# Scores of the experts as eight more columns of the value and output projections, in an attention and mixture-of-experts layer on one core

## The chip, the cores and the metric

The kernel runs on one core of a Trainium2 chip. The metric is device time in microseconds of one execution, lower is better. The engines that the profile names are TensorE (PE, with its weight loads as PEld), VectorE (DVE), ScalarE (ACT), GpSimd (POOL) and SyncE (SP), which issues most of the DMAs.

## The reference

Two sublayers, each fed with a normalised input, and each with its output normalised before it is added to the residual stream. `x` is 2 x 2048 x 256 in float32, with 4 heads of 64 and 8 experts of 256 x 256.

```python
x = L0_attn_x
x = x + _layernorm(_L0_attn_ref(_layernorm(x, axis=-1), ln_gamma, ..., w_o, b_o), axis=-1)
x = x + _layernorm(_L0_ffn_ref(_layernorm(x, axis=-1), gate_w, expert_w), axis=-1)

# _L0_attn_ref
xn = _layernorm(x, ln_gamma, ln_beta)
q, k, v = proj(w_q), proj(w_k), proj(w_v)          # each xn @ w.T
qn = _rmsnorm(q, q_gamma) * dh ** (-0.5); kn = _rmsnorm(k, k_gamma)
attn = softmax(einsum('bhid,bhjd->bhij', qn, kn))
return merge(einsum('bhij,bhjd->bhid', attn, v)) @ w_o.T + b_o

# _L0_ffn_ref
scores = einsum('bsh,eh->bse', x, gate_w)
onehot = one_hot(argmax(scores, axis=-1), E)
return x + einsum('bsef,bse->bsf', einsum('bsh,efh->bsef', x, expert_w), onehot)
```

Each token goes to the one expert with the highest score. Only the order of a token's eight scores matters, not their size.

## The kernel before

The 4096 tokens are 32 tiles of 128, 16 a batch. Two paths stand behind a branch on the size of the gammas of q and k (`bounded`, computed from `gq_all` and `gk_all`); the inputs take `bounded_path`, and the other path is not run.

Ahead of the branch the weights of q and k are loaded and turned on PE (`turn_weight`, line 148, copied by ACT at line 151), and the constants are made on POOL. `load_x` (line 70) loads four token tiles at a time on SP's queue; the first two of these loads are ahead of the branch.

`bounded_path` records its instructions in an order written out by hand. A generator stands for each job (`project` for a token tile, `tokens` for a tile behind the attention, `expert_weights`, `order`, `places`, `collect`, `block_sums`), and a `yield` ends the piece of work that it puts into one slot. `queue` holds each job with the slot in which it begins; `between(now)` moves every running job by one piece. A slot of the attention is two of the 256 steps: eight score matmul records `s` (line 953), their exponentials `p` on ACT (line 961), DVE's running sum `acc` of the exponentials (lines 996 and 998), and eight records `po` that weigh the values (line 1007). What `between` adds stands between a slot's `s` and its `po` on PE. The engines run their instructions strictly in the order in which they are recorded.

`project` normalises a tile of x, turns it on PE (`pt_x`, line 349), brings it back with ln_gamma and ln_beta as scale and bias on ACT (`xnT`, line 354, one instruction for each half), multiplies it by the weights of q and k (`pqk`, line 364) and of v (`pv`, line 373), and normalises and turns q and k. Tiles of the first batch fill the stretch before the first scores and the first slots; those of the second batch are spread over later slots. `turn_values` and `turn_rest` turn w_v, w_o and gate_w in the first slots (lines 148 and 167).

`tokens` takes a tile when its 512 rows have been attended: output projection `py` (line 700), bias (line 715), layer norm, residual sum `x2`, second layer norm `x2n` (line 731). Then it turns `x2n` (`pt_f`, line 739), copies it back (`xT`, line 747), multiplies it by the gate (`pg`, line 751), and `choose` (lines 176 to 183) makes the one-hot `pick` of the first best score.

Tiles 0 to 15 are group A and 16 to 27 group B. When the last tile of a group has its pick, `order` sorts the group's tokens by expert (`rank`, `src`, some 30 DVE instructions between them), and each `places` job then gathers 128 tokens of one expert (line 605), loads that expert's matrix (line 619), multiplies (`pt_g`, `pe`, lines 627 and 637), normalises and stores them; each `collect` job gathers a tile's results back (line 675) and adds the residual (line 687). The last four tiles, 28 to 31, have no group: they are multiplied by all eight experts (`pe`, line 776) and the picks select (lines 791 and 793).

When the attention is over, `finish` orders what is left by a list schedule with written-out costs: each job gives the engine and an estimate of its next piece in `Next(engine, cost, ...)`, and the piece that can begin first goes next.

Of the kernel before, what the change touches and what calls it, by code (L numbers as in the profile page):

```python
# [9 lines left out]
F32 = mybir.dt.float32  # L10
# [10 lines left out]
GAMMA_MAX = 5.0  # L21


@with_exitstack
def kernel(
# [39 lines left out]
    def load_x(g, pool, tag="xg", bufs=2):  # L65
        if pool:
            xs[g] = pool.tile([P, XG, D], F32, tag=tag, name=f"x{g}", bufs=bufs)
        else:
            xs[g] = xs[g - 2]
        nc.sync.dma_start(  # L70
            out=xs[g],
            in_=x_f[g * XG * P : (g + 1) * XG * P, :].rearrange("(c p) d -> p c d", p=P),
        )
# [5 lines left out]
    gk_all = const.tile([P, DH], F32, tag="gk_all", name="gk_all")  # L79
    nc.sync.dma_start(out=gq_all, in_=q_gamma.partition_broadcast(P))  # L80
# [8 lines left out]
    g_ln = const.tile([P, NCH], F32, tag="g_ln", name="g_ln")  # L89
    b_ln = const.tile([P, NCH], F32, tag="b_ln", name="b_ln")  # L90
    nc.sync.dma_start(out=g_ln, in_=ln_gamma.rearrange("(c p) -> p c", p=P))
    nc.sync.dma_start(out=b_ln, in_=ln_beta.rearrange("(c p) -> p c", p=P))
    load_x(1, store, "xg1", 1)
    early = ctx.enter_context(ExitStack())
    raw = early.enter_context(tc.tile_pool(name="raw_w", bufs=2))
    wq_raw = load_raw(raw, w_q, "wq_raw")
    wk_raw = load_raw(raw, w_k, "wk_raw")

# [7 lines left out]
    nc.gpsimd.memset(half, 0.5)  # L106
    ones = const.tile([P, DH], F32, tag="ones", name="ones")
# [30 lines left out]

    wqkT = const.tile([P, NCH, 2, D], F32, tag="wqkT", name="wqkT")
    wvT = const.tile([P, NCH, D], F32, tag="wvT", name="wvT")  # L140
    woT = const.tile([P, NCH, D], F32, tag="woT", name="woT")
    gateT = const.tile([P, NCH, E], F32, tag="gateT", name="gateT")

# [11 lines left out]
    )  # L155

    idle = psum_w.tile([P, P], F32, tag="idle", name="idle", bufs=1)
    for _ in range(18):
        nc.tensor.transpose(idle, ident, ident)
    for i, (w, name) in enumerate(((wq_raw, "pt_wq"), (wk_raw, "pt_wk"))):  # L160
        pt = psum_w.tile([P, KB // P, P], F32, tag="ps_w", name=name)
        turn_weight(w, pt, wqkT[:, :, i, :], nc.scalar.copy)
    early.close()

    def turn_gate(pt):
        for ic in range(NCH):
            nc.tensor.transpose(
                pt[:, ic, :E], gate_raw[:, ic * P : (ic + 1) * P], ident[:E, :E]
            )
        nc.vector.tensor_copy(gateT, pt[:, :NCH, :E])  # L170
# [15 lines left out]
    def bounded_path():  # L186
# [9 lines left out]
        wv_raw = load_raw(raw, w_v, "wv_raw", nc.sync)  # L196
# [25 lines left out]
        token = route.tile([P, NT], F32, tag="token", name="token")  # L222

        def four(ps):
            return ps.rearrange("p (a c) -> p a c", c=P)

        def turn_values():
            turn_weight(wv_raw, four(ps_m("pt_wv")), wvT)
            yield

        def turn_rest():
            nc.gpsimd.tensor_scalar(g_q8, g_q, DH**-0.5, None, ALU.mult)
            yield
            turn_weight(wo_raw, four(ps_m("pt_wo")), woT)
            turn_gate(four(ps_m("pt_gate")))
# [91 lines left out]
        class Batch:  # L327
            def __init__(self, b):
# [4 lines left out]
                self.V = kv.tile([P, NT, D], F32, tag="V", name=f"V{b}")  # L333

        def project(bt, t):
# [5 lines left out]
            mv, rs = moments(src, f"a{n}")  # L341
# [11 lines left out]
            for c in range(NCH):  # L353
                nc.scalar.activation(  # L354
                    xnT[:, c, :],
                    pt[:, c * P : (c + 1) * P],
                    AF.Identity,
                    bias=b_ln[:, c : c + 1],
                    scale=g_ln[:, c : c + 1],
                )  # L360
# [11 lines left out]
            for c in range(NCH):  # L372
                nc.tensor.matmul(  # L373
                    pv[:, :D],
# [7 lines left out]
            nc.scalar.copy(bt.V[:, t, :], pv[:, :D])  # L382
# [70 lines left out]
        def load_experts():  # L453
            nonlocal weD
            v = kv.tile([P, NT, D], F32, tag="V", name="ring")
            ring.extend(v[:, i : i + NCH, :] for i in range(0, NT, NCH))
# [237 lines left out]
        def tokens(bt, qb, j, oTs, gr):  # L694
# [3 lines left out]
            py = ps_m(f"py{tt}")[:, :D]  # L698
# [9 lines left out]
            if gr:  # L708
                y = wk.tile([P, D], F32, tag="y", name=f"y{tt}", bufs=3)
                xr = wk.tile([P, D], F32, tag="xr", name=f"xr{tt}")  # L710
            else:
                kept = wk.tile([P, HP, KB], F32, tag="p", name=f"kept{tt}", bufs=5)
                x2n, last = kept[:, 0, :D], kept[:, 0, D:]
                y, xr = kept[:, 1, D:], last
            nc.vector.tensor_tensor(y, py, bo, ALU.add)
# [6 lines left out]
            scale, _ = yield from norm(y, f"z{tt}", away, give="m")  # L722
            yield later("DVE", 1.2, give="m" if slot else "")

            x2 = wk.tile([P, D], F32, tag="x2", name=f"x2_{tt}", bufs=4)
            nc.vector.scalar_tensor_tensor(x2, y, scale, xr, ALU.mult, ALU.add)
# [5 lines left out]
            if gr:  # L732
                rows = slice((tt - gr.first) * P, (tt - gr.first + 1) * P)
                nc.sync.dma_start(out=gr.x2[rows, :], in_=x2)
                nc.sync.dma_start(out=gr.x2n[rows, :], in_=x2n)
            yield later("PE", 0.3, take="m")
# [6 lines left out]
            if gr:  # L743
                xT = wk.tile([P, NCH, P], F32, tag="xT", name=f"xT{tt}", bufs=4)
            else:
                xT = kept[:, 1, :D].rearrange("p (c n) -> p c n", n=P)
            nc.scalar.copy(xT, pt[:, :D].rearrange("p (c n) -> p c n", n=P))
            yield later("PE", 0.4, take="m", give="m")
            pg = ps_m(f"pg{tt}")
            for c in range(NCH):  # L750
                nc.tensor.matmul(  # L751
                    pg[:, :E],
                    xT[:, c, :],
                    gateT[:, c, :],
                    start=(c == 0),
                    stop=(c == NCH - 1),
                )
            yield then("DVE", 0.8)
# [679 lines left out]
```

## Time and profile before

| | |
|---|---|
| median of 3 runs | 821.41 us (819.0 to 821.75) |
| the profiled execution | 817.68 us, of which the span of instructions is 815.9 |
| granted TensorE clock, mean over the span | 0.982 |
| first scores `s` | 39.3 us |
| last `po` ends | 732.3 us |
| PE's last matmul ends | 799.5 us |
| `acc` on DVE, one 128x1024 addition | 1.222 us, 224 of them |
| `p` on ACT, one 128x1024 exponential | 1.110 us, 256 of them |

The profile's group lines give, for one line, engine, operation and shape, the count, the busy time and the mean of one instruction, then the engine's idle time before them and what ended it. A float32 matmul shows two records. PE's records overlap, so the distance from one start to the next is the better price of a job in a full slot. In the timeline, a start is followed by the time to the end of that run of equal instructions; brackets hold an idle time before it and its releaser.

### The profile page before, as it was taken

Reading aid. Unit: us, or ns where it says so; the run is one execution under the profiler, and the core shown is the slowest. Engines: PE = TensorE matmul, PEld = TensorE weight load, DVE = VectorE, ACT = ScalarE, POOL = GpSimd, SP = SyncE. Lnnn points to the kernel's source line nnn. Section 1 sums busy time; section 2 is a strip of 40 time slices with the busy share of each in tenths; the row PEclk is TensorE's granted clock in tenths of the full one; section 3 lists DMA queues with packets and bytes.
Section 4 is the critical chain, followed back from the end, with each engine's and each line's share of the span. In section 5 each row is a group of like instructions: output and inputs, shape, how many; then the busy total and the mean of one; then the engine's idle time right before and its main releaser. Section 6 shows DMA issues by size and latency. Waiting matters only on the chain.

```text
span 815.9 us, 10616 instructions
## 1 busy us (share of the span) xinstructions
PE 773.4 (95%) x3328; PEld 336.2 (41%) x3328; DVE 631.3 (77%) x1310; ACT 467.4 (57%) x759; POOL 321.9 (39%) x325
## 2 busy tenths in 40 slices
PE   6999999999999999999999999999999998987991
PEld 4544434433434443433333344444443333334650
DVE  3767788697869778787798978687787988977765
ACT  2776556666665665656645445656656555526750
POOL 3544412153443334242233026667563555236004
PEclk8999999999999999999999999999999999989996
DMA  4001111200100000010311033434221323267136
GB/s 151 27 27 39 52 53 52 65 27 20 46 20 19 20 14 20 7 33 20 103 59 46 18 106 97 125 101 115 72 59 53 98 91 116 78 192 224 50 112 195
DMA packets 48687, 57.60 MB, mean 71 GB/s; under 512 B 6408, under 2 KB 39952, under 8 KB 48624
## 3 DMA queue, kind: packets, MB, share of 16 engines
q1 hardware_dynamic: 42336, 44.91, 17.3%
q0 software_dynamic: 3568, 9.32, 4.6%
q10 hardware_dynamic: 2720, 2.62, 1.1%
q8 instruction: 28, 0.46, 0.2%
q14 instruction: 35, 0.29, 0.1%
HBM read 37.69 MB, written 19.14 MB: 70 GB/s over the span
## 4 chain that ended last, share of the span: by engine, by line
PE 75%; DVE 15%; ACT 3%; DMA 3%; issue 2%; POOL 1%; POOLq 0%; SPq 0%; DVEq 0%; ACTq 0%
PE po L1007 23%; PE s L953 23%; PE pqk L364 6%; DVE acc L998 5%; PE pv L373 3%; PE pe L776 3%; PE py L700 3%; PE peA L637 3%; PE sm L969 2%; DVE acc L977 2%; PE pt_qk L401 2%; PE peB L637 2%; PE pg L751 2%; PE pt_x L349 1%; PE pt_f L739 1%
## 5 line engine op out<-in xcount | busy, mean ns | idle before, releaser
L961 ACT ACTIVATE p<-s,nbound 128x1024 f32<-128x1024 f32 x256 | 271.3, 1110 | 214.6 <-PE s L953 205.1
L998 DVE TENSOR_TENSOR acc<-acc,p 128x1024 f32<-128x1024 f32 x224 | 273.7, 1222 | 12.1 <-ACT p L961 1.2
L953 PE MATMUL s<-QT,KT 64*128 64x512 f32 x1024 | 255.6, 618 | 0.6 <-ACT p L961 0.6
L1007 PE MATMUL po<-p,V 128*64 128x512 f32 x1024 | 250.2, 610 | 0.0
L953 PEld LDWEIGHTS s<-QT,KT 64*128 64x128 f32 x1024 | 88.6, 187 | 163.1 <-issue 96.7
L1007 PEld LDWEIGHTS po<-p,V 128*64 128x64 f32 x1024 | 64.1, 137 | 123.4 <-issue 122.5
L283 POOL TENSOR_TENSOR rn<-rs_t,mhalf 128x8 f32<-128x8 f32 x32 | 58.6, 1832 | 74.3 <-DVE rs_t L282 65.2
L283 POOL TENSOR_TENSOR rs_z<-rs_t,mhalf 128x1 f32<-128x1 f32 x28 | 35.9, 1283 | 86.6 <-DVE rs_t L282 86.6
L283 POOL TENSOR_TENSOR rs_a<-rs_t,mhalf 128x1 f32<-128x1 f32 x32 | 22.9, 715 | 105.6 <-DVE rs_t L282 105.6
L364 PE MATMUL pqk<-wqkT,xnT 128*128 128x512 f32 x128 | 62.6, 612 | 0.6 <-DVE woT L151 0.6
L605 POOL DMA_INDIRECT rows<-x2nA,srcA x23 | 30.7, 1334 | 41.1 <-DMA ring<-weTd 35.9
L283 POOL TENSOR_TENSOR rs_y<-rs_t,mhalf 128x1 f32<-128x1 f32 x28 | 32.7, 1167 | 33.0 <-DVE rs_t L282 32.8
L977 DVE RECIPROCAL acc<-acc 128x128 f32<-128x128 f32 x45 | 42.5, 945 | 0.0
L977 DVE RECIPROCAL acc<-sm 128x128 f32<-128x128 f32 x19 | 18.1, 954 | 26.0 <-PE sm L969 25.9
L675 POOL DMA_INDIRECT fgA<-fnA,posA x16 | 22.4, 1403 | 35.5 <-DVE rs_t L282 11.6
L700 PE MATMUL py<-woT,oT 128*128 128x256 f32 x128 | 34.7, 393 | 0.5 <-ACT xTB L632 0.5
L373 PE MATMUL pv<-wvT,xnT 128*128 128x256 f32 x128 | 32.9, 380 | 0.0
L373 PEld LDWEIGHTS pv<-wvT,xnT 128*128 128x128 f32 x128 | 24.6, 192 | 17.5 <-issue 12.0
L354 ACT ACTIVATE xnT<-pt_x,b_ln,g_ln 128x128 f32<-128x128 f32 x64 | 25.8, 459 | 8.4 <-PE pt_x L349 8.4
L605 POOL DMA_INDIRECT rows<-x2nB,srcB x19 | 19.8, 1044 | 26.9 <-DVE srcB L586 19.3
L283 POOL TENSOR_TENSOR rs_fA<-rs_t,mhalf 128x1 f32<-128x1 f32 x23 | 18.4, 800 | 28.5 <-DVE rs_t L282 28.0
L364 PEld LDWEIGHTS pqk<-wqkT,xnT 128*128 128x128 f32 x128 | 22.4, 195 | 17.4 <-issue 16.4
(234 smaller groups left out, 954.7 us busy)
## 6 DMA issues: line engine op xcount, KB each, us to landing
ring<-weTd SPq DMA_DIRECT2D x34, 256.0 KB, 3.0
x<-in_L_attn_x_dram SPq DMA_DIRECT2D x8, 512.0 KB, 4.2
xr<-in_L_attn_x_dram SPq DMA_DIRECT2D x28, 128.0 KB, 2.2
fnA<-fA SPq DMA_DIRECT2D x23, 128.0 KB, 2.4
fnB<-spare SPq DMA_DIRECT2D x18, 128.0 KB, 1.7
we_raw<-in_L_ffn_expert_w_dram ACTq DMA_DIRECT2D x8, 256.0 KB, 2.6
weTd<-weT SPq DMA_DIRECT2D x8, 256.0 KB, 2.1
x2A<-x SPq DMA_DIRECT2D x16, 128.0 KB, 1.7
```

Of the source, the lines that this page charges most:

```text
L283: nc.gpsimd.tensor_tensor(dst, t[:, :n], mhalf[:, :n], ALU.pow)
L354: nc.scalar.activation(xnT[:, c, :], pt[:, c * P : (c + 1) * P], AF.Identity, bias=b_ln[:, c : c + 1], scale=g_ln[:, c : c + 1],)
L364: nc.tensor.matmul(pqk, xnT[:, c, :], wqkT[:, c, :, :].rearrange("p a d -> p (a d)"), start=(c == 0), stop=(c == NCH - 1),)
L373: nc.tensor.matmul(pv[:, :D], xnT[:, c, :], wvT[:, c, :], start=(c == 0), stop=(c == NCH - 1),)
L605: nc.gpsimd.indirect_dma_start(out=xg, out_offset=None, in_=gr.x2n[:, :], in_offset=bass.IndirectOffsetOnAxis(ap=gr.src[:, j : j + 1], axi ...
L637: nc.tensor.matmul(pe, xT[:, c, :], w[:, c, :], start=(c == 0), stop=(c == NCH - 1))
L700: nc.tensor.matmul(py, oT[:, bass.ts(j, P)], woT[:, c, :], start=(c == 0), stop=(c == NCH - 1),)
L953: nc.tensor.matmul(s[:, r, :], bt.KT[rows, c, bass.ts(kc, P)], bt.QT[qb][rows, c, :], start=True, stop=True,)
L961: nc.scalar.activation(p, s, AF.Exp, bias=nbound)
L977: nc.vector.reciprocal(acc[:, 0, cols], share[:, cols])
L998: nc.vector.tensor_tensor(acc, acc, p, ALU.add)
L1007: nc.tensor.matmul(po[r * DH : (r + 1) * DH, :], batches[b].V[:, kc, h * DH : (h + 1) * DH], p[:, r, :], start=(kc == 0), stop=(kc == NT - 1),
```

## The change

The score of expert e for a token is the product of row e of gate_w with `x2n`. As `x2n` is `x2` less its mean, times a positive factor that all eight scores share, the order of the scores is that of the products of `x2` with the rows of gate_w from which their mean is taken (`gate_c`). `x2` is a sum of the attention's normalised output and of the normalised input, both linear in tensors that the kernel has before: so the changed kernel adds eight columns to the transposed weights of the output projection (`woT`, the product of w_o with the gate) and eight to those of the values (`wvT`, the gate itself), carries them along, and joins them at the end: score = y[256:264] x weight + V[256:264], with weight the ratio of the two scales (`roots` keeps the scale of each token's first norm).

For V's eight columns to be those of the bare normalised input, ln_gamma and ln_beta are no longer applied to it; they go into the weights. `xnT` is `xn` plus a constant 1/16, one ACT instruction for both halves, and `add_shares` rewrites the weights of q, k and v with `share` (128x128 tiles of (16 beta - gamma)/256), one PE product and one DVE instruction for each half. The product of the constant with the rewritten weights gives beta's part.

Of group tiles, `pt_f`, `xT` and `pg` go; the last four tiles keep `pt_f` and `xT`, and lose `pg`. The pick stands right behind `x2`, so a group is complete some slots earlier. `turn_outputs` takes the place of `turn_rest`'s weights and runs in slot 1; w_v is loaded and turned ahead of the branch; g_ln and b_ln are loaded first, and the second load of x behind the branch. The condition for the slots that sort their jobs by age changes.

```diff
+RAISE = 1 / 16
...
+    nc.sync.dma_start(out=g_ln, in_=ln_gamma.rearrange("(c p) -> p c", p=P))
+    nc.sync.dma_start(out=b_ln, in_=ln_beta.rearrange("(c p) -> p c", p=P))
     nc.sync.dma_start(out=gq_all, in_=q_gamma.partition_broadcast(P))
     nc.sync.dma_start(out=gk_all, in_=k_gamma.partition_broadcast(P))
     load_x(0, store, "xg0", 1)
...
-    load_x(1, store, "xg1", 1)
+    xs[1] = store.tile([P, XG, D], F32, tag="xg1", name="x1")
...
-    raw = early.enter_context(tc.tile_pool(name="raw_w", bufs=2))
+    raw = early.enter_context(tc.tile_pool(name="raw_w", bufs=3))
     wq_raw = load_raw(raw, w_q, "wq_raw")
     wk_raw = load_raw(raw, w_k, "wk_raw")
+    wv_raw = load_raw(raw, w_v, "wv_raw")
...
+    dif = const.tile([P, NCH], F32, tag="dif", name="dif")
+    nc.gpsimd.tensor_scalar(dif, b_ln, 1.0 / RAISE, None, ALU.mult)
+    nc.gpsimd.tensor_tensor(dif, dif, g_ln, ALU.subtract)
+    nc.gpsimd.tensor_scalar(dif, dif, 1.0 / D, None, ALU.mult)
+    share = const.tile([P, NCH, P], F32, tag="share", name="share")
+    for c in range(NCH):
+        nc.gpsimd.tensor_scalar(
+            share[:, c, :], ident, 0.0, dif[:, c : c + 1], ALU.mult, ALU.add
+        )
+    nc.scalar.activation(gate_c, gate_raw, AF.Copy, scale=-1.0 / D, accum_out=off)
+    nc.scalar.activation(gate_c, gate_raw, AF.Identity, bias=off)
+    DG = D + E
...
+    for w, name, dst in (
+        (wq_raw, "pt_wq", wqkT[:, :, 0, :]),
+        (wk_raw, "pt_wk", wqkT[:, :, 1, :]),
+        (wv_raw, "pt_wv", wvT[:, :, :D]),
+    ):
         pt = psum_w.tile([P, KB // P, P], F32, tag="ps_w", name=name)
-        turn_weight(w, pt, wqkT[:, :, i, :], nc.scalar.copy)
+        turn_weight(w, pt, dst, nc.scalar.copy)
+    pt = psum_w.tile([P, KB // P, P], F32, tag="ps_w", name="pt_gate")
+    for ic in range(NCH):
+        nc.tensor.transpose(
+            pt[:, ic, :E], gate_c[:, ic * P : (ic + 1) * P], ident[:E, :E]
+        )
+    nc.scalar.copy(gateT, pt[:, :NCH, :E])
+    nc.scalar.copy(wvT[:, :, D:], pt[:, :NCH, :E])
...
+    def add_shares(w, ps):
+
+        n = w.shape[-1]
+        for c in range(NCH):
+            nc.tensor.matmul(
+                ps[:, :n], share[:, c, :], w[:, c, :], start=(c == 0), stop=(c == NCH - 1)
+            )
+        for c in range(NCH):
+            nc.vector.scalar_tensor_tensor(
+                w[:, c, :], w[:, c, :], g_ln[:, c : c + 1], ps[:, :n], ALU.mult, ALU.add
+            )
+    def turn_outputs(w, ps, turned):
+        pt = four(ps("pt_wo"))
...
+        nc.vector.tensor_copy(woT[:, :, :D], pt.rearrange("p (i o) c -> p i (o c)", i=NCH))
+        pg = ps("pt_wog")
...
+        nc.vector.tensor_copy(
+            woT[:, :, D:], pg[:, : NCH * E].rearrange("p (c e) -> p c e", e=E)
+        )
+        pb = four(ps("pt_bo"))
+        for c in range(NCH):
+            nc.tensor.transpose(pb[:, c, :], bo[:, c * P : (c + 1) * P], ident)
+        nc.scalar.copy(turned, pb[:, :NCH, :])
+        pb = ps("pt_bias")
...
+        nc.gpsimd.tensor_copy(bias_o[:, :D], bo)
+        nc.vector.tensor_copy(bias_o[:, D:], pb[:, :E])
...
-            for c in range(NCH):
-                nc.scalar.activation(
-                    xnT[:, c, :],
-                    pt[:, c * P : (c + 1) * P],
-                    AF.Identity,
-                    bias=b_ln[:, c : c + 1],
-                    scale=g_ln[:, c : c + 1],
-                )
+            nc.scalar.activation(
+                xnT,
+                pt[:, :D].rearrange("p (c n) -> p c n", n=P),
+                AF.Identity,
+                bias=raised,
+            )
...
-                    pv[:, :D],
+                    pv[:, :DG],
...
-            py = ps_m(f"py{tt}")[:, :D]
+            py = ps_m(f"py{tt}")[:, :DG]
...
-            nc.vector.tensor_tensor(y, py, bo, ALU.add)
+            nc.vector.tensor_tensor(y, py, bias_o, ALU.add)
...
-            scale, _ = yield from norm(y, f"z{tt}", away, give="m")
-            yield later("DVE", 1.2, give="m" if slot else "")
+            scale, _ = yield from norm(y[:, :D], f"z{tt}", away, give="m")
+            yield later("DVE", 2.1, give="m" if slot else "")
...
+            nc.vector.scalar_tensor_tensor(x2, y[:, :D], scale, xr, ALU.mult, ALU.add)
+            weight = small.tile([P, 1], F32, tag="weight", name=f"weight{tt}")
+            nc.vector.tensor_tensor(weight, scale, roots[:, tt : tt + 1], ALU.mult)
+            score = small.tile([P, E], F32, tag="score", name=f"score{tt}")
+            nc.vector.scalar_tensor_tensor(
+                score, y[:, D:], weight, bt.V[:, qb * QT4 + j, D:], ALU.mult, ALU.add
+            )
+            pick = choose(small, score, tt, gr and gr.picks[:, tt - gr.first, :])
+            if gr:
+                gr.met += 1
+                if gr.met == gr.T:
+                    queue.append((now, order(gr)))
+                    queue.sort(key=lambda q: q[0])
             scale, shift = yield from norm(x2, f"y{tt}")
...
                 nc.sync.dma_start(out=gr.x2n[rows, :], in_=x2n)
+                return
             yield later("PE", 0.3, take="m")
...
-            yield later("PE", 0.4, take="m", give="m")
-            pg = ps_m(f"pg{tt}")
...
-            pick = choose(small, pg[:, :E], tt, gr and gr.picks[:, tt - gr.first, :])
-            yield later("PE", 3.8, take="" if gr else "s", give="m", order=2)
-            if gr:
...
-                return
+            yield later("PE", 3.8, take="s", give="m", order=2)
...
-            if now < NT + 4:
+            if 3 < now < NT + 4 or now == 2:
                 due.sort(key=lambda g: max(2 - now + begun[g], -1) % 4)
...
-        queue.append((2, turn_values()))
-        queue.append((3, turn_rest()))
+        queue.append((0, weights()))
+        queue.append((3, scale_g()))
+        queue.append((10, turn_rest()))
```

`weights` calls `add_shares` for q and k together and then for v, one in each piece; the first of its pieces is empty. The path that is not run gets the same weights.

## The prediction

> **What bounds the kernel now.** I read the page's shares and chain first, then TensorE's timeline slot by slot, then busy time by window, then both ends of the span.
>
> ```profile
> PE 773.4 (95%) x3328; PEld 336.2 (41%) x3328; DVE 631.3 (77%) x1310; ACT 467.4 (57%) x759; POOL 321.9 (39%) x325
> ...
> PE 75%; DVE 15%; ACT 3%; DMA 3%; issue 2%; POOL 1%; POOLq 0%; SPq 0%; DVEq 0%; ACTq 0%
> ```
>
> TensorE (PE) holds three quarters of the chain that ended last, VectorE (DVE) most of the rest. PE's timeline in the attention, slot by slot (start, duration, line, operation):
>
> ```profile
> 192.38 1.99 PE L953 MATMUL s<-QT,KT 64*128 64x512 f32 x8
> 194.30 1.94 PE L1007 MATMUL po<-p,V 128*64 128x512 f32 x8
> 196.17 1.99 PE L953 MATMUL s<-QT,KT 64*128 64x512 f32 x8
> ...
> 429.72 1.99 PE L953 MATMUL s<-QT,KT 64*128 64x512 f32 x8
> 431.64 0.61 PE L751 MATMUL pg<-gateT,xT 128*128 128x8 f32 x4
> 432.11 0.41 PE L739 MATMUL pt_f<-ident,x2n 128*128 128x128 f32 x2
> 432.45 1.94 PE L1007 MATMUL po<-p,V 128*64 128x512 f32 x8
> 434.32 1.99 PE L953 MATMUL s<-QT,KT 64*128 64x512 f32 x8
> ```
>
> An empty slot takes 196.17 - 192.38 = 3.79 us, one with a `pg` and a `pt_f` 434.32 - 429.72 = 4.60: the two jobs that the change takes away stand between matmuls that never wait, at 0.81 a token tile. Busy time by window (PE, weight load, DVE, ACT, POOL, clock, DMA) says who else is near the limit:
>
> ```profile
> 200.00:320.00 120.00, 120.00 (x522) 49.33 (x519) 98.19 (x186) 73.36 (x110) 45.10 (x36) 1.00 0.07 22
> 660.00:726.00 66.00, 60.96 (x271) 24.06 (x272) 61.14 (x135) 29.72 (x34) 23.46 (x26) 0.96 0.34 103
> 732.30:799.50 67.20, 60.13 (x224) 35.72 (x222) 46.01 (x161) 42.31 (x134) 19.23 (x20) 1.00 0.47 138
> ```
>
> From 200 to 320 PE is full and DVE at 82%. From 660 to 726, where four tiles come close together and a group is sorted, DVE is at 93%. The sort of group A, from the timeline:
>
> ```profile
> 468.44 3.94 PE L579 MATMUL srcA<-idsA,inrowA 128*128 128x23 f32 x32 [1.97 <-DVE inrowA L569]
> ...
> 471.42 1.12 ACT L961 ACTIVATE p<-s,nbound 128x1024 f32<-128x1024 f32 x1 [4.64 <-DVE acc L998]
> ```
>
> PE waits there for the sort, and then ScalarE (ACT) for DVE's late additions. The two ends, from the timeline and the DMA issues:
>
> ```profile
> 14.33 3.62 PE L364 MATMUL pqk<-wqkT,xnT 128*128 128x512 f32 x4
> ...
> 20.28 1.98 PE L364 MATMUL pqk<-wqkT,xnT 128*128 128x512 f32 x4 [0.57 <-DVE woT L151]
> ```
> ```profile
> gate_raw<-in_L_ffn_gate_w_dram POOLq DMA_DIRECT2D x1, 8.0 KB, 7.6
> ```
> ```profile
> 785.63 13.90 PE L776 MATMUL pe<-weD,kept 128*128 128x512 f32 x32
> ...
> 811.95 0.48 DVE L687 SCALAR_TENSOR_TENSOR fgB<-fgB,awayB 128x256 f32<-128x256 f32 x1 [0.99 <-DMA fgB<-fnB,posB]
> ```
>
> The first product runs at half the clock of the second (3.62 against 1.98 us). PE ends at 799.5, and 16.4 us of collecting rows follow.
>
> **The change part by part.** Where instructions stand is read from the order in which both programs, as built, issue them on each engine.
>
> *Taken from PE in the attention.* 28 tiles lose `pt_f` and `pg`. A `pg` costs 0.44 to 0.47 wherever it stands (409.72 to 415.01 with `pg` and `py`, 5.29; 415.01 to 419.86 with `py` alone, 4.85). A lone `pt_f` costs 0.37 (slot 4.16 at 175.81, against 3.79); beside another job 0.22 (7.17 at 217.60 against 6.96 at 168.85), since the change of operand is paid anyway. Tiles 0 to 11: 12 x 0.445 + 6 x 0.37 + 6 x 0.22 = 8.9. Tiles 16 to 23: 8 x 0.445 + 2 x 0.37 + 6 x 0.22 = 5.6. Tiles 12 to 15 and 24 to 27 stand where DVE is near full; PE alone would gain 3.0 and 3.1.
>
> *What DVE gets.* Per tile `weight` (128x1, nearest the 0.15 to 0.17 of small operations), `score` (128x8 with three inputs, like `tied`, 0.226) and eight columns in `y` (0.416 x 8/256 = 0.01): 0.41. In 200:320, some 5.5 tiles: DVE 98.2 + 2.3 in 120 - 4.4 us = 87%. It hides under PE, and the 8.9 and 5.6 hold. If that cover were gone, 28 x 0.41 = 11.5 would be on the path.
>
> *The sorts.* Each moves four slots ahead (rank 75 to 71, sources 78 to 74; for B 123 to 119 and 126 to 122), as do the places and collects behind it, with their gathers on POOL and expert loads on SP. The same sort then falls nearer the tokens' work, and a block's reciprocals (4 x (0.95 + 0.29)) come between rank and sources. A gain here ends where DVE fills the stretch: the twelve slots from 415.0 to 475.6 hold 55.6 of DVE in 60.6, with 4 x 0.41 then 57.2, so at most 3.4; 660:726 holds 61.1, then 62.8, of 66, so at most 3.2. The sort waits for its own chain besides, so what is late next is `srcA` and `srcB` again. I take 2.0 and 1.5. Bounds: from PE's side 3.0 + 1.97 of waiting = 5.0 and 3.1 + 5.0 (66 - 60.96) = 8.1 if DVE's backlog is worked off later; below, 0 and -1 if the sort waits a slot more.
>
> *ACT.* It loses 28 `xT` copies (0.375) and half of `xnT` (2 x 0.459 become one, nearest 0.48): 10.5 + 14 us of an engine 57% busy; nothing, hidden by PE.
>
> *Wider products.* `pv` and `py` go from 256 to 264 columns: 256 records x 0.216 x 8/256 = 1.7 us on PE. V's copy and `y` grow by 3%, hidden.
>
> *The start.* On SP, `g_ln` and `b_ln` (0.55 and 1.1 us of issue) go ahead of the gammas and `x0`, which lands about 1.5 us later than 9.1; `x1` goes behind the branch, is needed only at 20.2, and costs nothing; w_v goes to ACT's queue. POOL makes `share` before the branch (3 small, 2 of 128x128, nearest 0.32): hidden, since ACT is later. On ACT `gate_c` stands between the copies of w_q and w_k and waits for `gate_raw`, which lands at 4.85 + 7.6 = 12.45. Behind it: the w_k copy (0.59), then the second `gate_c`, on which PE's `pt_gate` and its branch wait; so `shares_qk` starts near 14.5. It is four records of 0.43 warm or 0.85 at the clock of 14.33, and ends at 16.2 to 17.9; DVE rewrites `wqkT` (2 x 0.69), PE does `shares_v` meanwhile, and `pqk` of tile 0 starts at 18 to 20 instead of 14.33. Tile 1 started only at 20.28, and follows now at 21.1 to 24.8: +0.8 to +4.5, taken +2.5, as part of the warming moves from `pqk` to the shares. From there tiles follow every 3.3 us as before.
>
> The Trainium skill ("TensorE: Matmul & The Clock Gate", Part 1) says that PE falls to half clock after an idle window of about 3.4 us and needs as long a busy one to return, which speaks against a chain of small waits ahead of the first product. The rows agree in kind (0.85 against 0.43 a record); with one more cold window by that rule the start would cost 1.7 more.
>
> *Moved into slot 1.* `pt_wo` (0.53), `pt_wog` (4 x 0.112), `pt_bo` (0.22) and `pt_bias` (0.45): 1.65, of which `pt_bias` waits for an ACT copy behind exponentials: +2.2, from 1.7 to 3.2.
>
> *After the attention* (732.3 to the end, 83.6). PE loses 4 `pg` (1.8); two places (2.2) run before the last `po`; but `sm127`, at which the last four tiles begin, stands behind places 1 and 2 and their transposes: +3 of waiting. PE's end: -1. At the very end 6 blocks of experts' products (6 x 3.44 = 20.6) follow the last place instead of 4 (13.9), so the first round of collects runs beneath them; what stays is tile 31 (4 x 0.5, norm 1.4, 0.6, 0.48 and 4.05 of landing = 8.5) or the last collect (gather 1.0, 4.45, 0.48, 4.05 = 10): 9.4 in place of 16.4, so -7. Together -8, from -13 to +3.
>
> **Sum:** -8.9 - 5.6 - 2.0 - 1.5 + 1.7 + 2.5 + 2.2 - 8.0 = -19.6. The profiled execution took 817.7 (span 815.9), which gives 798; it was 3.7 below the median of 821.4, so against that median 802.
>
> **The rivals.** (a) *DVE becomes the bound of the whole attention.* For: 93% in 660:726. Against: 82% in 200:320, and four slots hold 20.36 us with 16.8 of DVE (175.81 to 196.17); after the change 19.55 with 17.2. It decides from 2.4 us more per tile than my 0.41, or where its work arrives in bursts that five `p` buffers don't cover. Then none of PE's 20.6 is seen and DVE's 11.5 is: 821.4 + 11.5 + 1.7 + 2.5 + 2.2 - 8 = 831, slower.
>
> (b) *PE's slots don't shrink*, since busy matmuls overstate PE; the gain is then at the end alone: 821.4 + 6.4 - 8 = 820. Against it: 3.79 and 4.60 are distances between starts, no modelled ends. The skill ("Perfetto Trace Analysis", Identifying the Most-Contended Engine) calls matmul busy time a bad measure and prefers weight-load share, 41% here; by that rule DVE at 77% is first and the sum is that of (a) or (b). The distances decide for me.
>
> (c) *The end gains nothing* and both sorts give all back: 821.4 - 8.9 - 5.6 + 6.4 = 813. For: `sm127` is later, and two sorts are bound by DVE already.
>
> (d) *Everything goes through*, sorts 13 and end 13: 821.4 - 8.9 - 5.6 - 13.1 + 6.4 - 13 = 787.
>
> **How the numbers follow.** Forecast (790 to 809) 0.62; (c), up to 818, 0.20; (d) 0.06; (b) 0.04; (a) 0.08. The range 790 to 816 holds the forecast and most of (c). Within 0.3% (819 to 824, about what the runs' own spread can't tell from no change) lies (b), 0.04; slower 0.08; faster 0.88.
>
> **What would show it.** Slots with nothing between them stay at 3.79, and those of tiles 0 to 11 fall to what is left in them; DVE in 200:320 at 85 to 89%; `pqk` of tile 1 at 21 to 25; idle before `srcA` and `srcB` still there; PE's last matmul 8 to 13 us before the end. I am wrong if empty slots grow beyond 3.79 with ACT waiting for `acc`, if the first scores come over 8 us later than 39.3, or if the stretch behind the last `po` grows.

## The result and the profile after

The changed kernel takes 806.93 us (median of 4 runs, 805.89 to 808.12), the kernel before 821.58 in the runs beside it: a ratio of 0.983, 95% interval 0.980 to 0.986. The prediction was 802, from 790 to 816. The profiled execution took 805.99, of which the span is 804.2, 11.7 less than the span of before.

The page of after, busy time by engine and the chain of waits:

```profile
PE 760.8 (95%) x3166; PEld 320.4 (40%) x3166; DVE 639.4 (80%) x1379; ACT 448.8 (56%) x699; POOL 326.2 (41%) x336
...
PE 75%; DVE 12%; ACT 3%; DMA 3%; issue 3%; POOL 2%; SPq 0%; DVEq 0%; POOLq 0%; ACTq 0%
```

PE is still the bound, with 12.6 us less work; DVE has 8.1 more. PE's timeline in the attention (start, duration, line, operation):

```profile
408.37 1.99 PE L1040 MATMUL s<-QT,KT 64*128 64x512 f32 x8
410.28 1.16 PE L793 MATMUL py<-woT,oT 128*128 128x264 f32 x4
411.37 1.94 PE L1094 MATMUL po<-p,V 128*64 128x512 f32 x8
413.24 1.13 PE L1040 MATMUL s<-QT,KT 64*128 64x512 f32 x4
...
427.86 1.99 PE L1040 MATMUL s<-QT,KT 64*128 64x512 f32 x8
429.77 1.94 PE L1094 MATMUL po<-p,V 128*64 128x512 f32 x8
431.64 1.99 PE L1040 MATMUL s<-QT,KT 64*128 64x512 f32 x8
```

An empty slot still takes 3.78, and one with `py` takes 413.24 - 408.37 = 4.87, where before had 5.29 with `pg` and `py`. Busy time by window in after (length, PE, weight load, DVE, ACT, POOL, clock, DMA), then the two stretches of the sorts in before:

```profile
200.00:320.00 120.00, 120.00 (x504) 46.46 (x504) 99.46 (x194) 72.18 (x102) 47.00 (x36) 1.00 0.07 23
413.24:474.12 60.88, 55.97 (x249) 21.47 (x247) 57.14 (x127) 28.83 (x31) 19.84 (x20) 0.97 0.24 70
654.27:719.16 64.89, 57.74 (x241) 20.91 (x239) 59.47 (x135) 28.83 (x31) 23.22 (x25) 0.92 0.32 97
727.44:793.59 66.15, 56.25 (x192) 32.71 (x192) 47.69 (x172) 38.84 (x122) 25.41 (x27) 0.97 0.56 164
```
```profile
415.01:475.62 60.61, 58.65 (x270) 23.69 (x268) 55.58 (x120) 29.61 (x34) 14.43 (x16) 0.97 0.19 57
661.89:725.77 63.88, 58.84 (x262) 23.34 (x261) 59.05 (x131) 29.72 (x34) 23.23 (x26) 0.96 0.34 103
```

From 200 to 320 PE is full as before, and DVE's 99.46 us (83%) lie beneath it. In the sorts' stretches (slots 66 to 77 and 114 to 125) PE lost 2.7 and 1.1 us of work, DVE now has more than PE in both (in before by 0.2 us in the second alone), and neither stretch became shorter.

Where the 11.7 us come from, stage by stage in the two profiles:

| stage | before | after | difference | predicted |
|---|---|---|---|---|
| to the first slot | 41.9 | 43.6 | +1.7 | +2.5 |
| slot 0, with `turn_outputs` | 10.7 | 15.2 | +4.5 | +2.2 |
| slots 1 to 17 | 112.1 | 112.4 | +0.3 | part of +1.7 |
| slots 18 to 65 (tiles 0 to 11) | 250.3 | 242.1 | -8.25 | -8.9, rest of +1.7 |
| slots 66 to 77 (sort of A) | 60.6 | 60.9 | +0.3 | -2.0 |
| slots 78 to 113 (tiles 16 to 23) | 186.3 | 180.2 | -6.1 | -5.6 |
| slots 114 to 125 (sort of B) | 63.9 | 64.9 | +1.0 | -1.5 |
| slot 126 to the last `po` | 6.6 | 8.3 | +1.7 | none |
| behind the last `po` | 83.6 | 76.8 | -6.8 | -8 |

Each column is one execution, and some stages differ between kernels that leave them alone. gate_last, split_outputs and old_first_order (below), whose edits touch the start and the first slots only, take 62.5, 62.8 and 64.2 in slots 66 to 77 and 79.8, 79.8 and 78.3 behind the last `po`, where after has 60.9 and 76.8. In slots 18 to 65 all three take 242.1, and 180.1 to 180.3 in 78 to 113, as after does.

### The profile page after: what moved, and what is told of

Same layout as the page of the kernel before. It is cut to its first block, busy times and chain, and to the rows that moved or that the text cites. A ratio compares the mean times of both kernels' runs of the same rounds, so it can differ in the third digit from the quotient of the medians.

```text
span 804.2 us, 10268 instructions
## 1 busy us (share of the span) xinstructions
PE 760.8 (95%) x3166; PEld 320.4 (40%) x3166; DVE 639.4 (80%) x1379; ACT 448.8 (56%) x699; POOL 326.2 (41%) x336
## 4 chain that ended last, share of the span: by engine, by line
PE 75%; DVE 12%; ACT 3%; DMA 3%; issue 3%; POOL 2%; SPq 0%; DVEq 0%; POOLq 0%; ACTq 0%
PE s L1040 24%; PE po L1094 24%; PE pqk L454 7%; PE pv L463 4%; DVE acc L1085 3%; PE peA L730 3%; PE py L793 3%; PE pt_qk L491 2%; PE sm L1056 2%; PE peB L730 1%; PE pt_x L441 1%; DVE acc L1064 1%; PE pe L862 1%; DMA fgA<-fnA,posA 1%; ACT p L1048 1%
## 5 line engine op out<-in xcount | busy, mean ns | idle before, releaser
L1094 PEld LDWEIGHTS po<-p,V 128*64 128x64 f32 x1024 | 64.1, 138 | 129.2 <-issue 126.9
L374 POOL TENSOR_TENSOR roots<-rs_t,mhalf 128x1 f32<-128x1 f32 x32 | 23.9, 748 | 96.4 <-DVE rs_t L373 96.3
L837 ACT ACTIVATE x2n<-x,shift_y,rs_y 128x256 f32<-128x256 f32 x28 | 16.8, 599 | 44.0 <-POOL shift_y L391 39.2
L793 PE MATMUL py<-woT,oT 128*128 128x264 f32 x128 | 35.6, 402 | 0.5 <-ACT xTB L725 0.5
L768 POOL DMA_INDIRECT fgA<-fnA,posA x16 | 19.9, 1243 | 37.9 <-DVE rs_t L373 12.0
L463 PE MATMUL pv<-wvT,xnT 128*128 128x264 f32 x128 | 33.7, 386 | 0.0
L471 ACT COPY qk<-pqk 128x512 f32<-128x512 f32 x32 | 18.8, 587 | 22.8 <-PE pqk L454 22.8
```

The lines of the kernel that those rows point to most:

```text
L374: nc.gpsimd.tensor_tensor(dst, t[:, :n], mhalf[:, :n], ALU.pow)
L463: nc.tensor.matmul(pv[:, :DG], xnT[:, c, :], wvT[:, c, :], start=(c == 0), stop=(c == NCH - 1),)
L768: nc.gpsimd.indirect_dma_start(out=o, out_offset=None, in_=gr.fn[:, :], in_offset=bass.IndirectOffsetOnAxis(ap=gr.pos[:, t : t + 1], axis= ...
L793: nc.tensor.matmul(py, oT[:, bass.ts(j, P)], woT[:, c, :], start=(c == 0), stop=(c == NCH - 1),)
L1094: nc.tensor.matmul(po[r * DH : (r + 1) * DH, :], batches[b].V[:, kc, h * DH : (h + 1) * DH], p[:, r, :], start=(kc == 0), stop=(kc == NT - 1),
```

## Experiments

Each kernel is the changed one with one edit. The ratio is to the kernel before on the same chip; those without one were timed once, and are read by stages.

| kernel | time, us | before beside it | ratio, 95% interval |
|---|---|---|---|
| gate_kept | 818.2 | 820.4 | |
| score_twice | 808.2 | 820.4 | |
| split_outputs | 808.1 | 820.4 | 0.985, 0.981 to 0.989 |
| sort_plus2 | 821.0 | 820.4 | 1.000, 0.997 to 1.003 |
| sort_plus5 | 813.3 | 821.5 | 0.989, 0.985 to 0.994 |
| gapA2 | 808.2 | 821.5 | 0.984, 0.979 to 0.989 |
| old_first_order | 810.0 | 821.5 | |
| gate_last | 807.9 | 821.5 | |
| warm_src | 817.7 | 831.3 | 0.985, 0.979 to 0.990 |
| yields_warm | 825.5 | 831.3 | 0.994, 0.991 to 0.996 |
| copy_first | 805.1 | 820.4 | 0.982, 0.977 to 0.988 |
| copy_first_b | 805.3 | 820.4 | 0.982, 0.977 to 0.987 |

### gate_kept: the old gate's work put back beside the new

```diff
+                pt = ps_m(f"pt_f{tt}")
...
+                nc.scalar.copy(xT, pt[:, :D].rearrange("p (c n) -> p c n", n=P))
...
+                pg = ps_m(f"pg{tt}")
...
                 return
```

The 28 group tiles do `pt_f`, `xT` and `pg` again; the picks don't use them.

> The changed kernel, but its 28 group tiles still run the old turn of x2n, its copy and the product with the gate, with the result unused. Theory (the gain is PE's time in full slots): the slots of tiles 0 to 11 grow back by 8 to 9.5 us in all, those of tiles 16 to 23 by 5 to 6, the stretches of the two sorts by 0 to 3 each, and the whole by 13 to 20 us. Rival (matmul busy time overstates PE, the slots don't care): 0 to 2 us in all.

PE's timeline of gate_kept, one slot with `pt_f` and one with `pg`:

```profile
409.95 1.99 PE L1061 MATMUL s<-QT,KT 64*128 64x512 f32 x8
411.87 0.44 PE L845 MATMUL pt_f<-ident,x2n 128*128 128x128 f32 x2
...
414.96 1.99 PE L1061 MATMUL s<-QT,KT 64*128 64x512 f32 x8
416.88 0.61 PE L854 MATMUL pg<-gateT,xT 128*128 128x8 f32 x4
417.35 1.14 PE L793 MATMUL py<-woT,oT 128*128 128x264 f32 x4
418.42 1.94 PE L1115 MATMUL po<-p,V 128*64 128x512 f32 x8
420.28 1.99 PE L1061 MATMUL s<-QT,KT 64*128 64x512 f32 x8
```

A slot with `pg` and `py` is at 420.28 - 414.96 = 5.32 again, against 4.87 without `pg`. By stages, against after: slots 18 to 65 +9.5, 66 to 77 +1.5, 78 to 113 +6.25, 114 to 125 -2.4, behind the last `po` -0.3. What the two jobs cost on PE is near what their removal gave, in the slots of tiles 0 to 11 and 16 to 23. At the sorts it isn't, and the whole falls short of what was expected: +11.3 in one run, where 13 to 20 were. PE at rank A (brackets hold an idle time and its releaser):

```profile
444.63 0.46 PE L579 MATMUL rankA<-picksA,before 128*128 128x128 f32 x2 [1.95 <-DVE picksA L271]
```

PE waits 1.95 us for the picks here and 4.16 in after, 2.29 and 5.16 at rank B: at the sorts, the time that the change takes off PE becomes a longer wait for DVE. The rival that PE's slots don't shrink falls.

### score_twice: DVE's new work doubled

```diff
+            nc.vector.tensor_tensor(weight, scale, roots[:, tt : tt + 1], ALU.mult)
+            nc.vector.scalar_tensor_tensor(
+                score, y[:, D:], weight, bt.V[:, qb * QT4 + j, D:], ALU.mult, ALU.add
+            )
```

> The changed kernel, with weight and score of each token tile computed twice (two more small DVE instructions a tile, 0.38 us, 12 us in all). Theory (DVE hides under PE but for the stretches of the two sorts and the end): 2 to 4 us slower, nothing in the slots of tiles 0 to 11. Rival (DVE is the bound of the whole attention): 10 to 12 us slower, spread evenly.

Busy time in 200 to 320, score_twice:

```profile
200.00:320.00 120.00, 119.66 (x503) 46.59 (x502) 101.50 (x202) 71.80 (x101) 47.68 (x37) 1.00 0.07 23
```

The product in the edit's first line also says what `weight` is: the product of the two norms' factors. DVE has 2.0 us more in this window. Slots 18 to 65 grow by 0.8, 66 to 77 by 2.2, 106 to 113 by 0.9, no other stage by more than 0.3; the 2.2 gives 63.1, which is inside the spread of 60.9 to 64.2 given above. PE's waits at the ranks are clearer: 5.98 and 6.89 us, where after and the five other kernels with the same slots and the same jobs ahead of both sorts have 4.14 to 4.18 and 5.16 to 5.17. So DVE's new work is nearly hidden where PE is full, and shows at the sorts as a longer wait of PE. That DVE bounds the whole attention falls: the whole grew by 1.2 in one run.

### split_outputs: slot 1's new work spread over four slots

```diff
+        yield
         pg = ps("pt_wog")
...
+        yield
         pb = four(ps("pt_bo"))
...
+        yield
         pb = ps("pt_bias")
```

> The changed kernel, with the four parts of turn_outputs put into four pieces of successive slots instead of one. Theory (of the 4.5 us by which slot 0 grew, 1.7 are work, the rest is waiting for ACT's copy of the turned bias and a half-clock window behind thin matmuls): 2 to 3 us faster, no half-clock window near 49 us. Rival (it is all work, or the half-clock comes with the thin matmuls wherever they stand): 0 to 1 us.

Slot 0 takes 12.7 and the slots behind it 1.5 more, together some 14.2. In gate_kept, score_twice and seven others, which do all in one slot as after does, slot 0 takes 13.5. So spreading wins nothing; of after's 15.2, 1.7 belongs to one window of half clock, which those profiles lack, and the rest is PE's work and its waits.

### sort_plus2, sort_plus5, gapA2: the sorts later, the picks earlier

```diff
-                    queue.append((now, order(gr)))
+                    queue.append((now + 2, order(gr)))
```

sort_plus5 has 5 in place of 2, and puts the sorts where before had them (ranks in slots 74 and 122, sources in 77 and 125; after 70, 118, 73 and 121; sort_plus2 71, 119, 74 and 122). gapA2 leaves the sort and spaces A's last four tiles:

```diff
-                    gap = 1 if last else 4 if following else 1
+                    gap = (2 if gr.name == "A" else 1) if last else 4 if following else 1
```

> The changed kernel, with both sorts begun two slots later. Theory A (the sorts now begin before DVE has made the last picks, and PE's wait at rank, 4.2 and 5.2 us with half-clock time behind it, is lost): the wait at rank goes, the stretches of the sorts shrink by 2 to 5 us each, and the whole is 3 to 8 us faster. Theory B (DVE is full there, wherever the sort stands): the stretches keep their length within 1 us, two places of group B go back behind the last po, and the whole is 0 to 3 us slower.

> The changed kernel, with both sorts in the slots in which the kernel before has them (rank in 74 and 122, sources in 77 and 125). If the earlier place is what cost the sorts' stretches the PE time that they were to gain: 66 to 78 takes 57 to 59 us instead of 60.9, 114 to 126 takes 59 to 62 instead of 64.9, no wait at rank. If DVE's content decides wherever the sort stands: both stay within 1 us. If the early places of group B are what shortened the stretch behind the last po: it takes 81 to 86 us again instead of 76.8; if the shorter chain of the last four tiles did it: 75 to 78.

> The changed kernel, with the last four tiles of group A begun two slots apart instead of one, so that their DVE work doesn't pile up ahead of the sort. Theory (a backlog of DVE, some 6 us of tokens' work and additions a slot of 4.9, makes PE wait at rank): no wait at rank of group A, the stretch 66 to 78 takes 57 to 59 us, everything behind it unchanged, the whole 2 to 4 us faster. Rival (the sort's own chain is what PE waits for): within 1 us.

In after the sort waits for the last pick. The timeline of after:

```profile
437.79 0.77 PE L579 MATMUL rankA<-picksA,before 128*128 128x128 f32 x2 [4.16 <-DVE picksA L271]
...
453.06 3.75 PE L672 MATMUL srcA<-idsA,inrowA 128*128 128x23 f32 x32
...
456.10 0.48 ACT L1068 COPY acc<-sm 128x384 f32<-128x384 f32 x1 [7.13 <-DVE acc L1064]
```

None of the three kernels waits so at rank A, and none gains by it: slots 66 to 77 take 67.1 (sort_plus2), 62.7 (sort_plus5) and 63.9 (gapA2), against 60.9 in after and 62.5 to 64.2 in the three kernels named above, with DVE's work the same within 0.7 us (57.1 to 57.8). In gapA2 and sort_plus5 PE waits 4.09 and 1.97 us at `srcA` instead. So taking away the wait for the picks alone brings nothing, and in sort_plus2 what follows is worse: it loses the whole gain (1.000), which neither theory had. At B sort_plus5 takes 68.3, where after has 64.9. The end moves as well: behind the last `po` sort_plus5 takes 83.7, where before has 83.6, and gapA2, gate_last and old_first_order on the same chip, which sort B where after does, have 78.3 to 79.8. No place of group B runs ahead of the last `po` in sort_plus5, as in before; in after and those three two do. So moving the sorts alone undoes the end's gain.

### old_first_order, gate_last: the start

```diff
-            if 3 < now < NT + 4 or now == 2:
+            if now < NT + 4:
```

> The changed kernel, with the old condition for the order of jobs in the first slots. If the new order is worth something: the first scores come 1 to 4 us later, from products behind waits. If not: within 0.5 us, and all else equal.

PE in old_first_order:

```profile
19.63 0.69 PE L441 MATMUL pt_x<-ident,xn 128*128 128x128 f32 x2 [2.33 <-DVE xn L437]
20.11 3.21 PE L454 MATMUL pqk<-wqkT,xnT 128*128 128x512 f32 x4
```

The first scores come at 43.2, against 41.1 in after and 39.9 to 41.6 in the other experiments: PE waits 2.33 for `xn`, falls to half clock, and `pqk` takes 3.21. The new order of the first pieces is worth some 2 us (1.5 to 3.3 against the other kernels, one execution each).

gate_last moves the two `gate_c` instructions on ACT behind the copies of the three weights.

```diff
-    nc.scalar.activation(gate_c, gate_raw, AF.Copy, scale=-1.0 / D, accum_out=off)
-    nc.scalar.activation(gate_c, gate_raw, AF.Identity, bias=off)
...
+    nc.scalar.activation(gate_c, gate_raw, AF.Copy, scale=-1.0 / D, accum_out=off)
+    nc.scalar.activation(gate_c, gate_raw, AF.Identity, bias=off)
     pt = psum_w.tile([P, KB // P, P], F32, tag="ps_w", name="pt_gate")
```

> The changed kernel, with both instructions for gate_c recorded behind the weights' copies, so that the second copy no longer waits for gate_raw on ACT. Theory (the start is a chain over gate_raw, w_k's copy and the shares): shares_qk starts 0.3 to 1 us earlier than 12.4. Rival (the branch behind the gate's own turn holds PE): no change.

`shares_qk` starts at 12.31, against 12.38 in after: the place of `gate_c` costs nothing. The first scores are 1.1 earlier, which is inside the 39.9 to 41.6 of the others; the first window of half clock ends at 16.7 and not at 17.9.

### warm_src, yields_warm: half clock behind narrow matmuls

```diff
             ps = ps_m(f"src{n}")
+            warm = ps_m(f"warm{n}")
             for t in range(T):
+                nc.tensor.transpose(warm[:, :P], ident, ident)
```

The same transpose stands before each product of `pt_wog`. yields_warm has one more `yield` before the rank and one more before the sources as well.

> One transpose of the identity (128 columns) stands before each of the narrow matmuls of the two sorts (23 and 19 columns, 16 and 12 of them) and of the gate's product in slot 1 (8 columns, 4 of them). Theory: a stretch of 3.4 us filled by matmuls of few columns is followed by half clock though PE is busy in it (eight profiles so far show such a window behind the sources with no idle time of PE in it). Then no window at half clock that follows such a stretch with less than 0.5 us of idle time is seen behind srcA, srcB or slot 1; those behind the waits for the ranks stay. The time is after's 806.9 plus up to 16 x 0.22 = 3.5 and 12 x 0.22 = 2.6 for the transposes, less 1.7 for each window that goes: 804 to 812. Rival: the windows come from the sorts' waits or from the phase of something else; they stay behind the sources with no idle time before them.

> The same transposes, and rank and sources one and two slots later, so that neither has to wait for DVE's chain. Theory A (the stretches of the sorts are bound by DVE's work, 57.2 us from slot 66 to 77, whatever waits are taken away): no wait at the ranks above 1 us, but slots 66 to 77 stay at 59 or above, and the kernel is at 805 to 812. Theory B (the waits at the ranks and the half clock behind them cost the stretch its gain): slots 66 to 77 fall to 57 or below and those from 114 to 125 to 62 or below, and the kernel is at 799 to 804.

Windows of 3.4 us with the sources and behind them, in before (sort of A), in after (sort of B; PE's busy time is the second figure, the clock the third from the end), and in warm_src (sort of B):

```profile
468.50:471.90 3.40, 3.40 (x31) 3.40 (x31) 3.30 (x5) 0.48 (x1) 0.00 (x0) 0.99 0.75 230
471.90:475.30 3.40, 3.40 (x11) 1.12 (x10) 3.19 (x4) 0.63 (x1) 0.00 (x0) 0.50 0.72 202
```
```profile
697.20:700.60 3.40, 3.40 (x28) 2.95 (x28) 3.30 (x5) 1.07 (x2) 0.00 (x0) 1.00 0.73 201
700.60:704.00 3.40, 3.40 (x10) 0.99 (x8) 3.26 (x6) 1.43 (x2) 1.08 (x1) 0.50 0.77 219
```
```profile
698.25:701.65 3.40, 3.40 (x38) 3.40 (x36) 3.21 (x4) 1.58 (x3) 0.00 (x0) 1.00 0.64 224
701.65:705.05 3.40, 3.40 (x18) 1.28 (x17) 3.35 (x5) 1.07 (x2) 1.48 (x2) 1.00 0.74 215
```

PE is busy all the time in each first line, and yet the clock is halved in the next 3.4 us of before and after; with a transpose before each narrow product it is not, in either sort of either kernel. Slot 1 says nothing on this, as of the kernels without a transpose there only after has half clock behind it. The transposes cost little: the sources of B take 3.54 us from first to next in place of 2.79.

It isn't the whole of the loss. In warm_src the stretches take 62.4 and 64.4; its total, on a chip where before takes 831.3, stands to before as after's does. Its last `po` ends at 727.4 us, as in after; the stretch behind takes 86.0 in place of 76.8, and as there is no profile of before from that chip, what lengthens it stays open. In yields_warm, which has no wait for the picks either, they take 66.5 and 67.6, although DVE's work is 57.4 in the first: more than theory A's bound explains. Its timeline names the wait:

```profile
455.81 0.48 ACT L1074 COPY acc<-sm 128x384 f32<-128x384 f32 x1 [10.20 <-DVE acc L1070]
...
457.36 3.78 PE L1046 MATMUL s<-QT,KT 64*128 64x512 f32 x8 [6.55 <-ACT p L1054]
```

`block_sums` copies a block's sums on ACT, and this copy waits for DVE's first reciprocal, which stands behind the sort's chain. The exponentials are queued on ACT behind the copy, so PE waits for them. sort_plus2 has the same two waits, 10.20 and 6.55.

### copy_first, copy_first_b: that wait taken away

```diff
+            if early_copy:
+                nc.scalar.copy(acc[:, 0, P:], sm[:, P:])
             for j in range(QT4):
                 cols = bass.ts(j, P)
                 nc.vector.reciprocal(acc[:, 0, cols], share[:, cols])
...
-                    nc.scalar.copy(acc[:, 0, P:], sm[:, P:])
+                    if not early_copy:
+                        nc.scalar.copy(acc[:, 0, P:], sm[:, P:])
```

`early_copy` holds from a group's last pick to its sources. Both kernels have the transposes between the narrow products of the sorts; copy_first starts the rank one slot later.

> Ranks one slot later than in after (as in sort_plus2: 71 and 119, sources 74 and 122), the transposes of warm_src between the narrow matmuls, and during a sort ACT's copy of the block's sums stands ahead of DVE's first reciprocal, so that it no longer waits for DVE. Theory: what sort_plus2 and yields_warm lost in the stretch is one wait, ACT's copy behind a reciprocal that stands behind the sort's chain on DVE (10.2 us of ACT and 6.55 us of PE in yields_warm), and the half clock that it brings. Then the copy's wait falls below 2 us, PE's wait for p in slots 72 to 75 below 3, and slots 66 to 77 take 58 to 61 in place of sort_plus2's 67.1. Rival: DVE's lateness itself holds the exponentials (five buffers of p, freed by acc); then only the name of the waiting instruction changes, and the slots stay at 64 to 67.

> The ranks where after has them, with the transposes and the copy ahead of the reciprocal during a sort. Theory: in after the loss is the wait for the picks (4.2 and 5.2 us) and half clock, and ACT's wait of 7.1 us is hidden by the sources' matmuls; so the copy changes little: slots 66 to 77 at 60.5 to 62.5 (warm_src 62.4), 114 to 125 at 63.5 to 64.5 (64.4), the kernel within 0.5% of after. Rival: ACT's wait is what bounds these slots; then 66 to 77 fall below 59.5.

copy_first, ACT's timeline and then the windows of slots 66 to 77, 114 to 125 and from the last `po` to PE's end:

```profile
443.97 0.50 ACT L1069 COPY acc<-sm 128x384 f32<-128x384 f32 x1
```
```profile
411.25:469.47 58.22, 55.56 (x262) 21.47 (x261) 54.72 (x125) 28.45 (x30) 19.84 (x20) 1.00 0.25 73
649.89:712.90 63.01, 55.99 (x250) 20.50 (x248) 58.94 (x136) 28.68 (x30) 25.98 (x26) 0.97 0.36 104
720.27:792.58 72.31, 62.51 (x199) 34.62 (x198) 48.54 (x174) 40.63 (x126) 25.72 (x27) 0.91 0.51 149
```

The copy no longer waits, PE's waits for `p` shrink to 0.88 and 1.62, there is no half clock in the first stretch, and slots 66 to 77 take 58.2, slots 114 to 125 63.0: 2.7 and 1.9 less than after. The rival, that DVE's lateness itself holds the exponentials, falls.

The 58.2 is below every other kernel's; the 63.0 isn't (gate_kept has 62.5), so a gain at B is not shown. DVE holds 54.72 us in the first stretch, 2.4 less than in after: two of its additions fall behind the stretch, and slots 78 to 113 take only 0.3 more for it. The later rank and the copy are both needed: sort_plus2 and yields_warm have the later rank without the copy's move (67.1 and 66.5).

copy_first_b, whose ranks wait for the picks as in after, stays at 61.8 and 64.1, as expected: there the wait for the picks is the loss, and the copy's wait taken away changes nothing.

copy_first's last `po` is 7.2 us earlier than after's (4.5 of it in the sorts' stretches, 1.7 in the window of half clock that after has in slot 0, 0.9 in the place that no longer runs ahead of it), but its total isn't measurably better (0.982 against 0.983). From the last `po` to PE's end it takes 72.3 in place of 66.2. One place of B instead of two runs before the last `po`, and the clock is at half from 745.9 to 759.6. How much of the 6 us each of the two explains wasn't tried; copy_first_b, with two places ahead of the last `po`, takes 69.3 on the same chip.

## Why the prediction was right, step by step

**PE's slots: right.** Tiles 0 to 11 were to give 8.9 less a part of the 1.7 for wider products, and gave 8.25; tiles 16 to 23 were to give 5.6, and gave 6.1. gate_kept takes both back (9.5 and 6.25). The distance between starts in a full slot priced the jobs to within some 12%. The wider products: `pv` and `py` records follow at 0.223 in place of 0.216, the price that was put on them.

**DVE hidden: right.** Forecast 85 to 89% of 200 to 320, measured 83, a little below; score_twice shows that doubling the work costs 0.8 us in all of slots 18 to 65. The Trainium skill ("Perfetto Trace Analysis", Identifying the Most-Contended Engine) judges TensorE by its share of peak arithmetic (MFU) and its weight-load share instead of matmul busy time. By the latter, 41% here, DVE with its 77% comes first; gate_kept decides against that order in this kernel.

**The sorts: mis-sized.** Predicted -2.0 and -1.5, measured +0.3 and +1.0. The mechanism named, DVE fills the stretch, is part of it: DVE's work passed PE's (57.14 against 55.97). But the step "at most 3.4" took the room as gain, and the wait was expected in the wrong place: at `srcA` and `srcB`, as in before. After has no idle time there, and 4.16 and 5.16 us at the ranks. The sort follows the last pick directly, so PE, in order, waits there for DVE's lateness, and gate_kept shows that this wait took up the time that PE was freed of; once the sort is one slot later (sort_plus2, yields_warm), ACT waits behind DVE's chain with the copy of the block's sums. With both gone copy_first has 58.2 and 63.0: the gain forecast for A was there to be had (-2.4 against before); that for B (-0.9) is inside the spread.

**Slot 1's work: mis-sized.** Predicted +2.2 (1.7 to 3.2), measured +4.5, in the slot counted as 0 here. PE's timeline of after:

```profile
46.34 0.96 PE L231 MATMUL pt_wog<-gateT,wo_raw 128*128 128x8 f32 x8
...
48.18 0.61 PE L247 MATMUL pt_bias<-gateT,turned 128*128 128x8 f32 x4 [0.46 <-ACT turned L244]
48.65 1.09 PE L491 MATMUL pt_qk<-ident,qk 128*128 128x128 f32 x4
49.53 3.15 PE L454 MATMUL pqk<-wqkT,xnT 128*128 128x512 f32 x4
```

`pqk` takes 3.15 where the next slot's takes 1.88: a window of half clock behind the narrow products, 1.7 us; why it falls in after alone stays open. Without that window the slot takes 13.5 in other profiles, +2.8, inside the range given. In the sum of work, `pt_wog` was taken as four records of 0.112; it shows eight, 0.94 from first to next, which is 0.5 more.

**The start: right in kind, somewhat less.** Predicted +2.5 (0.8 to 4.5), measured +1.7. PE in after:

```profile
12.38 3.75 PE L209 MATMUL shares_qk<-wqkT,share 128*128 128x512 f32 x4 [0.57 <-ACT wvT L202]
...
18.00 1.88 PE L454 MATMUL pqk<-wqkT,xnT 128*128 128x512 f32 x4
...
22.13 1.98 PE L454 MATMUL pqk<-wqkT,xnT 128*128 128x512 f32 x4 [0.28 <-ACT xnT L445]
```

`pqk` of tile 0 was to start at 18 to 20, of tile 1 at 21.1 to 24.8. The gate's weights landed 2.5 us earlier than taken from before, so `shares_qk` began at 12.4 and not 14.5; gate_last shows that the place of `gate_c` on ACT doesn't matter.

**The end: right, with one term on the wrong side.** The size, -6.8, is that of one execution; the three kernels that leave the end alone stand 3.7 to 5.2 below before. From the last `po` PE takes 66.15 in place of 67.2, -1 as predicted; the collects behind PE's end take 10.6 in place of 16.4, forecast 9.4. PE's timeline of after at the end:

```profile
773.45 20.14 PE L862 MATMUL pe<-weD,kept 128*128 128x512 f32 x46
```

These 20 us follow the last place; in before it was 13.90, so the first round of collects lies beneath them, as forecast. But the two places were booked off the end and not onto the slots where they now run: the attention's last slots grow by 1.7 (by 0.8 in copy_first, with one place there).

**The rivals.** (a) and (b) fell to score_twice and gate_kept. (c), end without gain and both sorts giving all back, was right in its half on the sorts; sort_plus5 shows that the end did gain. Against the spans the sum of -19.6 missed by 7.9 us: sorts 4.8, slot 1 2.3, the places 1.7 and the end 1.2, less 0.8 at the start, 0.5 at tiles 16 to 23 and 0.75 at tiles 0 to 11 with the wider products. Against the medians it missed by 5, as the profiled execution of before lay below its median by more than that of after: some 3 us of the nearness to 802 are luck.

## What to carry to other kernels

Price a job in a full, in-order engine by the distance between starts in slots with and without it; that held here to within some 12%. Where a change moves a burst of dependent work (a sort) to another slot, list the instructions that will stand behind it on every engine and what is queued behind each of those: here one small ACT copy behind a reciprocal held PE for 6.5 us in sort_plus2 and yields_warm. When a piece of work goes from one end of a boundary to the other, book it on both sides.

## What the hardware showed unexpectedly

The half clock behind the sources isn't idleness. In all fourteen profiles, those of before and after among them, windows of half clock begin on a grid of 3.413 us (within 0.007 us inside one execution), whose phase differs from run to run. In the ten profiles without the transposes, a grid window without idle time of PE, at full clock, was followed by half clock where products of 19 or 23 columns filled 2.6 us of it or more (10 of 10), and never where they filled 2.3 or less. With a 128-column transpose before each product, windows that sources and transposes fill for 2.95 to 3.41 us weren't followed by half clock (6 of 6, in four kernels). (Worked out from the starts of the clock's changes and of the matmuls.)

Nor must a window be idle throughout. Of the windows at full clock behind the first 12 us, all 44 in which PE idled for 2.0 us or more were followed by half clock, 14 of the 40 with 1.5 to 2.0, and none with less but for the three in which the sources filled the rest (idle 1.2 to 1.5), the ten above and after's slot 0 (idle 0.46). Each window of half clock with PE full costs about 1.7 us (slot 0 takes 15.2 with it and 13.5 without), and whether one falls depends on the phase; it may be a part of the 2 to 3 us by which four executions of one kernel differ.

The Trainium skill ("TensorE: Matmul & The Clock Gate", Part 1) tells of a free-running window of this length, which the grid agrees with, and of half clock after an idle window; the rows above show it after a partly idle one and after a busy one too, so the measurement goes beyond the page.
